# An adaLN transformer block in f32 on one core: the opening of block 0 rearranged (weight sums on GpSimd, modulation ahead of the transposes)

## The chip, the core and the metric

The kernel runs on one core of a Trainium2 chip. A core has a matrix engine (TensorE, PE in the profile, with its weight loads as PEld), VectorE (DVE), ScalarE (ACT), GpSimd (POOL) and SyncE (SP), whose queue here issues nearly all DMAs. The engines run side by side and wait for each other at semaphores; each takes its own instructions strictly in the order in which they were written into its queue. SBUF holds 128 partitions of working memory, PSUM holds the results of TensorE in banks of 128 x 512 f32.

The metric is the device time of one execution in microseconds. A lower time is better.

## The reference

One transformer block over x of 8 x 1024 x 512, with a condition vector for each of the 8 sequences. Everything is f32.

```
mod = silu(condition) @ Wada + bada
sh_a, sc_a, gt_a, sh_m, sc_m, gt_m = split(mod, 6)
xn = layernorm(x) * g1 + be1
xm = xn * (1 + sc_a) + sh_a
q, k, v = split(xm @ Wqkv)                      # 16 heads of 32
attn = softmax(where(causal, q @ k.T * 32 ** -0.5, -inf))
x = x + gt_a * ((attn @ v) @ Wproj + bproj)
xn = layernorm(x) * g2 + be2
xm = xn * (1 + sc_m) + sh_m
x = x + gt_m * (gelu(xm @ W1 + b1) @ W2 + b2)
```

## The kernel before

The 8 x 1024 tokens are worked off as 16 blocks of 512 tokens (two to a sequence). For each block there is a row normalization, a transposition with the modulation (`xm`, four chunks of 128 features by 512 tokens), the three projections k, q and v, the attention in four groups of four heads, the output projection, and the MLP. The order of the instructions is written out by a small planner in Python: every instruction that it emits is noted with an estimated duration, and it picks among several threads of work (the linear work of `plan`, side threads such as the modulation of the next block, the attention) the one that could go on first. Nothing of the order is decided on the chip: each engine executes its own list.

The large linear steps use a Strassen-like scheme (`strassen`, L710): with the weight cut into quarters A11, A12, A21, A22 and the activations into B11, B21, B22 and four derived tiles, a projection takes seven products of 64 matmuls each instead of eight, in the order A11 B11, S2 T2, A12 B21, S1 T1, S3 T3, S4 B22, A22 T4. S1 to S4 are sums of weight quarters, T1 to T4 are differences of activation tiles. T1, T2 and T3 are made on VectorE, T4 on GpSimd (both through `modulated`, L568, with `either` at L148 choosing the engine for T3 and T4). A product's results go from a PSUM bank through `copy_out` (L179) or `combine_out` (L190).

The weight sums are made once. For k, q and v of block 0 (`raw_step`, L282) the four raw quarters are loaded, `weight_sums` (L661) makes S1 to S4, and `keep` (L656) writes each of them to DRAM; for all later blocks the sums are loaded from there. W1 and W2 get theirs from `preparation` (L676), which runs beside block 0.

The weight tiles come in through a ring of nine buffers (`fetch`, L318): a load is issued when the piece nine places earlier has been used for the last time. All loads and all keeps stand in SP's one queue, in the order in which the planner met them.

PSUM is divided into three banks for the linear work (`banks`, L163), a group of four banks `st` for scores and exponentials, and one bank for the attention's output.

What the opening does, in the order of `plan[-1]` (L229): four x tiles of block 0, the eight quarters of two modulation parts (each 256 KB) and then the quarters of k are loaded. The rows of block 0 are normalized (`normalize`, L528: statistics on VectorE, a square root on ScalarE in `root`, L546, and the application of scale and offset to four tiles on ScalarE in `apply`, L553). The step `("at", 0)` transposes them; for block 0 alone the sixteen transposes go into the four banks of `st` (the tile `early`, L610), so that they need no linear bank, and the modulation of their results waits until `norm_columns_a` (L434) has made the gain and shift columns. The step `("mod", 1)` is told to wait for those transposes (`"early"`, L411). Then come k, q, the transposes of block 1 and v.

Of the kernel before, what the change touches and what calls it, by code (L numbers as in the profile page):

```python
# [9 lines left out]
F32 = mybir.dt.float32  # L10
BF16 = mybir.dt.bfloat16
AF = mybir.ActivationFunctionType
# [10 lines left out]
def kernel(  # L23
# [33 lines left out]
    nc = tc.nc  # L57
# [167 lines left out]
    def mlp_steps(n):  # L225
        return [("u", n, i) for i in range(NQ)] + [("d", n, part) for part in range(4)]

    plan = {
        -1: [("at", 0), ("mod", 0), ("mod", 1), ("norm_columns_a",), ("load_xa", 1)]  # L229
        + [("k", 0), ("norm_a", 1), ("q", 0), ("at", 1), ("v", 0)],  # L230
        0: [("load_xa", 2), ("preps",), ("k", 1), ("norm_a", 2), ("gates", "a"), ("q", 1)]
        + [("mod", 3), ("at", 2), ("v", 1), ("mod", 4), ("k", 2), ("gates", "m"), ("columns_m",)],
    }
# [51 lines left out]
    def pieces_of(step):  # L285

        kind = step[0]
        if kind == "mod":
            return [(Wada, step[1], kh, fh) for kh, fh in RAW]
        if kind == "gates":  # L290
            return [(Wada, GATES[step[1]][0], kh, fh) for kh, fh in RAW]
        if kind == "proj":
            return [(Wproj, 0, k) for k in range(NC)]
        if kind == "d":
            return [
                (W2, i, *AT[a]) if a in AT else (W2, i, a)
                for a in DOWN_ORDER[step[2]]
                for i in range(NQ)
            ]
        if raw_step(step):  # L300
            return [(*source_of(step), kh, fh) for kh, fh in RAW]
# [92 lines left out]

    cond_act = tmp.tile([P, TB], F32, tag="top", name="cond_act", bufs=1)[:B, :]
    nc.scalar.activation(cond_act, cond_sb, AF.Silu)
    pc = banks[0][:, : NC * B].rearrange("p (c b) -> p c b", b=B)
    for c in range(NC):
        nc.tensor.transpose(pc[:, c, :], cond_act[:, ts(c, P)], ident[:B, :B])
# [8 lines left out]
    def modulation(i):  # L408
        at = take(4)
        part = {kf: halves(j) for kf, j in zip(RAW, at)}  # L410
        yield ["early"] if i == 1 else [], [BANK]  # L411
        bank = lin_bank()
        pm = banks[bank][:, : NC * B].rearrange("p (c b) -> p c b", b=B)
        for c in range(NC):
            for k in range(NC):
                w = part[k // 2, c // 2][:, k % 2, ts(c % 2, P)]
                matmul(pm[:, c, :], w, condT[:, k, :], k == 0, k == NC - 1, bank=bank)
                note("PE", 90)
                yield [], []
# [23 lines left out]
        return gain, shift  # L443

    columns_of = {}
    written["columns"] = written["early"] = NEVER
    gate_rows = {}

    kept_rows = {}
# [78 lines left out]
    def normalize(tiles, key, sources):  # L528

        for t in range(NTT):  # L530
            written["hat", key, t] = NEVER
        mv = small.tile([P, NTT, 2], F32, tag="mv", name=f"mv_{key}")
        rstd = small.tile([P, NTT], F32, tag="rstd", name=f"rstd_{key}")
        offset = small.tile([P, NTT], F32, tag="offset", name=f"offset_{key}")
        got = []

        def statistics(t):
            st = small.tile([P, nc.vector.BN_STATS_DIM], F32, tag="st", name=f"st_{key}_{t}")
            nc.vector.bn_stats(st, tiles[t])
# [12 lines left out]

        def apply():  # L553
            for t, xt in enumerate(tiles):
                xh = xt
                if key[0] == "m":
                    xh = tmp.tile([P, D], F32, tag="hat", name=f"xh_{key}_{t}", bufs=NTT)
                nc.scalar.activation(
                    xh, xt, AF.Identity, bias=offset[:, t : t + 1], scale=rstd[:, t : t + 1]
                )  # L560
                note_act(800, None, [("rstd", key)], [("hat", key, t)])
                got.append(xh)
            hats[key] = got

        for t in range(NTT):
            add_job(lambda t=t: statistics(t), [sources[t]], key[0] == "m")

    def modulated(key, b, guards):  # L568
# [16 lines left out]
        }  # L585
        xm_of[key] = part
        at = {t: (key, t) for t in part}

        def modulate(c, place, source):
            gain, shift = columns_of[key[0]]  # L590
            writes = [at["B11"], at["T1"]] if c < 2 else [at["B21"], at["B22"]]
            if sooner([source], writes, 770, 780) == "DVE":
                nc.vector.tensor_scalar(
                    xm[:, c, :], place, gain[:, c, b : b + 1], shift[:, c, b : b + 1],
                    ALU.mult, ALU.add,
                )
                note("DVE", 770, [source], writes)
            else:
                nc.scalar.activation(  # L599
                    xm[:, c, :], place, AF.Identity,  # L600
                    bias=shift[:, c, b : b + 1], scale=gain[:, c, b : b + 1],
                )
                note_act(780, None, [source], writes)
# [7 lines left out]
        for c in range(NC):  # L611
            if key != "a0":
                if c:
                    yield [("hat", key, 0)], [BANK]
                bank = lin_bank()
                place, source = banks[bank], ("l", bank)
            else:
                place, source = early[:, c, :], "st"
            for t in range(NTT):
                if t or c:  # L620
                    yield [("hat", key, t)], []
                nc.tensor.transpose(place[:, ts(t, P)], got[t][:, ts(c, P)], ident)  # L622
                note_pe(TR, "whole", [("hat", key, t)], [source])
            if key != "a0":
                modulate(c, place, source)
                live[bank] = False
        if key == "a0":
            written["early"] = 0.0
            yield ["columns"], []
            for c in range(NC):  # L630
                modulate(c, early[:, c, :], "st")
        nc.vector.tensor_tensor(part["T2"], part["B22"], part["T1"], ALU.subtract)  # L632
        note("DVE", 700, [at["B22"], at["T1"]], [at["T2"]], port=True)
        for out, a, b in (("T3", "T2", "B11"), ("T4", "B21", "T2")):
# [26 lines left out]
    def weight_sums(step, part):  # L661
# [3 lines left out]
        got = {"A11": part[0, 0], "A12": part[1, 0], "A21": part[0, 1], "A22": part[1, 1]}  # L665
        for j, (out, a, b, op) in enumerate(SUMS):
            got[out] = stage[:, j, :].rearrange("p (k n) -> p k n", n=HB)
            nc.vector.tensor_tensor(got[out], got[a], got[b], op)
# [28 lines left out]
    def run_preparation(everything=False):  # L697
        while prepared[0] is not None:
# [4 lines left out]
            try:  # L703
                prepared[0][1] = next(prepared[0][0])
            except StopIteration:
                prepared[0] = None

    tail_key = [None]

    def strassen(step, x, dest, target, row, done):  # L710
# [300 lines left out]
    def perform(step):  # L1011
# [2 lines left out]
            yield from modulation(step[1])  # L1014
        elif kind == "norm_columns_a":
            columns_of["a"] = norm_columns("a", 0, 1, O_G1, O_BE1)
            written["columns"] = 0.0
        elif kind == "gates":
            yield from gates(step[1])
        elif kind == "columns_m":  # L1020
# [20 lines left out]
        elif kind == "at":  # L1041
            n = step[1]
            guards = [("m used", n - 3)] if n > 2 else [("v done", 0)] if n == 2 else []
            start(modulated(f"a{n}", blocks[n][0], guards))
        elif kind == "mt":
            n = step[1]
            guards = [("v done", n + 1)]
            start(modulated(f"m{n}", blocks[n][0], guards))
# [492 lines left out]
```

## Time and profile before

| what | value |
|---|---|
| median of 3 runs | 3687.08 us (3687.07 to 3687.18) |
| the profiled execution | 3685.5 us |
| its span (first to last instruction) | 3683.6 us |
| mean granted TensorE clock | 0.992 |
| busy, share of the span: PE, DVE, ACT, POOL | 97%, 59%, 36%, 55% |
| DMA, mean over the span | 117 GB/s |

The opening of block 0 in the same execution, from its timeline:

| us from the start | what |
|---|---|
| 4.85 to 8.83 | SP issues the eight loads of the two modulation parts |
| 8.1 to 12.7 | PE: modulation part 0, as its weights land |
| 11.0 to 12.3 | ACT: table load for the square root |
| 13.0 to 16.0 | ACT: scale and offset applied to four row tiles |
| 13.9 to 19.1 | PE: sixteen transposes |
| 19.0 to 20.7 | PE: modulation part 1 |
| 20.8 to 21.7 | DVE: gain and shift columns |
| 21.8 to 24.6 | ACT: four modulated chunks |
| 22.7 | PE: first product of k |
| 28.5 | PE: second product of k |
| 53.8 | PE: end of q's last product |
| 60.6 to 64.2 | DVE: weight sums of v |
| 77.5 | PE: end of v's last product, k of block 1 begins |

How to read it: busy shares are taken over the whole span. PE's 97% says that it is seldom without an instruction, not that every instruction runs at full rate; the granted clock says that. The clock is granted in steps of 3.41 us, and a step is at full or at half rate. The profile prints it for any stretch as a mean.

### The profile page before, as it was taken

To read this page: it belongs to the slowest core of one execution; us is meant where nothing else is said; L and a number is where in the kernel's file an instruction comes from. 1 tells how busy PE (TensorE), PEld (TensorE's weight loads), DVE (VectorE), ACT (ScalarE), POOL (GpSimd) and SP (SyncE) were. 2 spreads that over 40 slices of the span, in tenths; PEclk is the share of its full clock that TensorE was granted. 3 is DMA by queue.
4 is the path that set the end of the run, shared out by engine and by line. 5 is a ranking of instruction groups with operands and counts; after the bars stand their busy time and mean duration, and the time that the engine had idled before them with its cause. 6 is when DMAs were issued, how large, how long until landed. Compare 5 with 4: busy or idle time off the path is not lost.

```text
span 3683.6 us, 121126 instructions
## 1 busy us (share of the span) xinstructions
PE 3578.0 (97%) x54821; PEld 1770.6 (48%) x54821; DVE 2158.7 (59%) x2455; ACT 1330.8 (36%) x1415; POOL 2030.0 (55%) x2052
## 2 busy tenths in 40 slices
PE   7979999999999999999999999999999999998989
PEld 4424445445454455544545454454544445454445
DVE  5756676564755647465564656646666465664542
ACT  2324334252343523335242352424524244341421
POOL 1676745656456563556636665356653556445661
PEclk9989999999999999999999999999999999999999
DMA  5642333434334343433434333343333433334334
GB/s 182 202 135 90 109 106 105 127 102 130 102 114 119 108 123 110 131 95 107 125 107 139 96 96 119 111 133 102 102 119 111 136 105 108 107 106 123 90 110 133
DMA packets 307893, 430.34 MB, mean 117 GB/s; under 512 B 25900, under 2 KB 176236, under 8 KB 307380
## 3 DMA queue, kind: packets, MB, share of 16 engines
q1 hardware_dynamic: 307264, 422.56, 38.2%
q8 instruction: 432, 7.08, 0.8%
q14 instruction: 81, 0.66, 0.1%
q10 hardware_dynamic: 116, 0.03, 0.0%
HBM read 394.12 MB, written 28.38 MB: 115 GB/s over the span
## 4 chain that ended last, share of the span: by engine, by line
PE 86%; DVE 7%; ACT 2%; POOL 2%; issue 2%; DMA 0%; SPq 0%; ACTq 0%; POOLq 0%; DVEq 0%
PE bank L199 58%; PE st L1292 8%; PE sc L1206 8%; PE po L1343 7%; DVE mx L1226 2%; PE st L1303 2%; PE bank L1361 2%; POOL pT L1427 1%; PE bank L622 1%; ACT pT L1315 1%; DVE hT L928 1%; DVE sc L1218 1%; DVE xr L156 1%; DVE t_m L156 1%; PE bank L1266 0%
## 5 line engine op out<-in xcount | busy, mean ns | idle before, releaser
L1427 POOL TENSOR_TENSOR pT<-pT,pT 128x512 f32<-128x512 f32 (+3 forms) x1280 | 1209.0, 979 | 550.1 <-ACT pT L1315 383.8
L1315 ACT ACTIVATE pT<-st 128x2048 f32<-128x2048 f32 (+1 forms) x320 | 546.6, 1708 | 1019.4 <-PE st L1303 956.9
L199 PE MATMUL bank<-w,hT 128*32 128x256 f32 x14336 | 808.7, 380 | 5.0 <-DVE hT L928 2.2
L1226 DVE TENSOR_REDUCE mx<-sc 128x4 f32<-128x2048 f32 (+3 forms) x384 | 669.0, 1756 | 208.2 <-PE sc L1206 201.6
L199 PEld LDWEIGHTS bank<-w,hT 128*32 128x32 f32 x14336 | 453.2, 110 | 357.9 <-issue 61.3
L199 PE MATMUL bank<-xm_m,w 128*32 128x256 f32 x8192 | 506.4, 380 | 0.8 <-DVE u_u L191 0.8
L1320 POOL TENSOR_SCALAR_AFFINE_SELECT pT<-pT 128x512 f32<-128x512 f32 x256 | 178.1, 708 | 575.2 <-ACT pT L1315 574.9
L199 PE MATMUL bank<-t_m,w 128*32 128x256 f32 x6144 | 383.1, 380 | 2.4 <-DVE t_m L632 1.0
L1292 PE MATMUL st<-qT,kT 32*128 32x512 f32 (+3 forms) x3072 | 342.9, 530 | 35.9 <-DVE mx L1226 34.7
L199 PEld LDWEIGHTS bank<-xm_m,w 128*32 128x32 f32 x8192 | 254.3, 110 | 249.3 <-issue 95.8
L1206 PE MATMUL sc<-kT,qT 32*128 32x512 f32 (+3 forms) x3072 | 340.2, 527 | 12.6 <-DVE mx L1226 6.5
L1343 PE MATMUL po<-pT,v 128*32 128x512 f32 (+3 forms) x3072 | 315.1, 497 | 6.5 <-POOL pT L1320 6.5
L1218 DVE TENSOR_TENSOR sc<-sc,mask 128x512 f32<-128x512 f32 (+1 forms) x192 | 168.0, 875 | 249.4 <-PE sc L1206 221.6
L199 PEld LDWEIGHTS bank<-t_m,w 128*32 128x32 f32 x6144 | 193.0, 110 | 174.3 <-issue 50.2
L199 PE MATMUL bank<-w,qT 128*32 128x512 f32 x2048 | 241.5, 598 | 6.1 <-POOL qT L1381 3.2
L199 PE MATMUL bank<-xm_a,w 128*32 128x256 f32 x3968 | 244.2, 382 | 2.0 <-ACT xm_a L599 2.0
L1376 DVE RECIPROCAL rec<-rec 128x128 f32<-128x128 f32 x256 | 223.7, 918 | 21.6 <-ACT rec L1367 21.6
L1292 PEld LDWEIGHTS st<-qT,kT 32*128 32x128 f32 x3072 | 129.7, 185 | 201.9 <-issue 60.6
L1206 PEld LDWEIGHTS sc<-kT,qT 32*128 32x128 f32 x3072 | 126.7, 184 | 176.0 <-ACT pT L1315 84.7
L191 DVE TENSOR_TENSOR hT<-bank,u_u 128x512 f32<-128x512 f32 x192 | 130.4, 686 | 120.4 <-PE bank L199 118.4
L199 PE MATMUL bank<-t_a,w 128*32 128x256 f32 x2944 | 186.6, 382 | 0.0
L1315 ACT ACT_TABLE_LOAD x88 | 112.9, 1283 | 183.5 <-PE st L1303 182.8
(184 smaller groups left out, 3546.8 us busy)
## 6 DMA issues: line engine op xcount, KB each, us to landing
w<-in_L_cond_W_dram SPq DMA_DIRECT2D x384, 256.0 KB, 2.9
w<-kept_up_S SPq DMA_DIRECT2D x256, 256.0 KB, 2.6
w<-kept_down_S SPq DMA_DIRECT2D x256, 256.0 KB, 2.7
w<-kept_qkv_S SPq DMA_DIRECT2D x180, 256.0 KB, 2.9
w<-in_L_cond_Wqkv_dram SPq DMA_DIRECT2D x147, 256.0 KB, 3.5
hat<-in_x_dram SPq DMA_DIRECT2D x64, 256.0 KB, 3.4
w<-in_L_cond_Wproj_dram SPq DMA_DIRECT2D x64, 256.0 KB, 3.4
xr<-in_x_dram SPq DMA_DIRECT2D x64, 256.0 KB, 4.4
```

The costliest lines, as they stand in the source:

```text
L156: nc.vector.tensor_tensor(out, a, b, op)
L191: nc.vector.tensor_tensor(out, src, other, op)
L199: nc.tensor.matmul(ps[r, :], lhsT[:, r], rhs, start=start, stop=stop, skip_group_check=True)
L1206: nc.tensor.matmul(sc[:, j, c0 : c0 + w], qTs[n][r, g, ts(qt, P)], keys_of(n, kh)[r, g, :w], start=True, stop=True, skip_group_check=True,)
L1218: nc.vector.tensor_tensor(diagonal, diagonal, mask[:, :span].unsqueeze(1).to_broadcast([P, HPG, span]), ALU.add,)
L1226: nc.vector.tensor_reduce(mx[:, kh, qt, :], sc[:, :, c0 : c0 + w], axis=AX.X, op=ALU.max)
L1292: nc.tensor.matmul(st[:, j, c0 : c0 + w], kT[r, g, ts(k % NTT, P)], qT[r, g, TB - w :], start=(c0 == 0), stop=False, skip_group_check=True,)
L1315: nc.scalar.activation(pT[:, :, :used], st[:, :, :used], AF.Exp, scale=scale)
L1320: nc.gpsimd.affine_select(diagonal, diagonal, pattern=[[0, HPG], [1, P]], compare_op=ALU.is_ge, fill=0.0, base=0, channel_multiplier=-1,)
L1343: nc.tensor.matmul(po[r, TB - w :], v[:, k % NTT, g * P + j * hd : g * P + (j + 1) * hd], pT[:, j, c0 : c0 + w], start=(k == 0), stop=last ...
L1376: nc.vector.reciprocal(some, some)
L1427: nc.gpsimd.tensor_tensor(into, into, pT[:, j, c0 : c0 + w], ALU.add)
```

## The change

The diff touches only the opening and the code that it shares with later blocks, whose own steps keep their order. It does this:

- `plan[-1]` is put in another order: both modulation parts first, then a new step `("sums", "k", 0)`, the columns, the transposes of block 0, the loads of block 1's rows, the sums of q, the projection k, and so on; the sums of v stand between q and the transposes of block 1.
- A weight's sums become a step of their own (`sum_weights`), which takes the ring's pieces, and `strassen` picks them up. They are made on GpSimd instead of VectorE. Their keeps move in SP's queue with them.
- An activation with the square root on one column (`warm`) is put behind the silu, so that the table is loaded there.
- Of block 0's four row tiles, two are scaled on VectorE.
- The transposes of block 0 go through the three linear banks like those of the later blocks, and the four-bank tile and its conditions (`early`, `columns`) go.

```diff
     plan = {
-        -1: [("at", 0), ("mod", 0), ("mod", 1), ("norm_columns_a",), ("load_xa", 1)]
-        + [("k", 0), ("norm_a", 1), ("q", 0), ("at", 1), ("v", 0)],
+        -1: [("mod", 0), ("mod", 1), ("sums", "k", 0), ("norm_columns_a",), ("at", 0)]
+        + [("load_xa", 1), ("sums", "q", 0), ("k", 0), ("norm_a", 1), ("q", 0)]
+        + [("sums", "v", 0), ("at", 1), ("v", 0)],
...
     nc.scalar.activation(cond_act, cond_sb, AF.Silu)
+    warm = const.tile([P, 1], F32, tag="warm", name="warm")
+    nc.scalar.activation(warm, eps, AF.Sqrt)
+    table[0] = "sqrt"
...
-        yield ["early"] if i == 1 else [], [BANK]
+        yield [], [BANK]
...
-                nc.scalar.activation(
-                    xh, xt, AF.Identity, bias=offset[:, t : t + 1], scale=rstd[:, t : t + 1]
-                )
-                note_act(800, None, [("rstd", key)], [("hat", key, t)])
+                if key == "a0" and t % 2:
+                    nc.vector.tensor_scalar(
+                        xh, xt, rstd[:, t : t + 1], offset[:, t : t + 1], ALU.mult, ALU.add
+                    )
+                    note("DVE", 700, [("rstd", key)], [("hat", key, t)])
+                else:
+                    nc.scalar.activation(
+                        xh, xt, AF.Identity, bias=offset[:, t : t + 1], scale=rstd[:, t : t + 1]
+                    )
+                    note_act(800, None, [("rstd", key)], [("hat", key, t)])
...
+        for c in range(NC):
+            if c:
+                yield [("hat", key, 0)], [BANK]
+            bank = lin_bank()
+            for t in range(NTT):
+                if t:
+                    yield [("hat", key, t)], []
+                nc.tensor.transpose(banks[bank][:, ts(t, P)], got[t][:, ts(c, P)], ident)
+                note_pe(TR, "whole", [("hat", key, t)], [("l", bank)])
...
-        if key == "a0":
-
-            early = ps_st.tile([P, NC, TB], F32, tag="st", name="early")
...
-            nc.vector.tensor_tensor(got[out], got[a], got[b], op)
-            note("DVE", 700, [], [("sums", *step, out)], port=True)
+            nc.gpsimd.tensor_tensor(got[out], got[a], got[b], op)
+            keys = [("sums", *step, x) for x in (a, b)]
+            note("POOL", 1290, keys, [("sums", *step, out)])
             keep(w, i, out, stage[:, j, :])
...
+    def sum_weights(step):
+        at = take(4)
+        part = {kf: halves(j) for kf, j in zip(RAW, at)}
+        w = weight_sums(step, part)
+        w.update({a: part[kf] for a, kf in AT.items()})
+        summed[step] = at, w
...
         if raw:
-            at = take(4)
-            part = {kf: halves(j) for kf, j in zip(RAW, at)}
-            w = weight_sums(step, part)
+            at, w = summed.pop(step)
```

More of the change, by code (lines that the diff above doesn't have):

```diff
@@ L299, in pieces_of @@
             ]
+        if kind == "sums":
+            return [(*source_of(step[1:]), kh, fh) for kh, fh in RAW]
         if raw_step(step):
-            return [(*source_of(step), kh, fh) for kh, fh in RAW]
+            return []
         if kind in ("k", "q", "v", "u"):
@@ L445 @@
     columns_of = {}
-    written["columns"] = written["early"] = NEVER
     gate_rows = {}
@@ L566, in normalize, with modulated @@
             add_job(lambda t=t: statistics(t), [sources[t]], key[0] == "m")
-    def modulated(key, b, guards):
+    def modulated(key, gain, shift, b, guards):
         for t in ("B11", "B21", "B22", "T1", "T2", "T3", "T4"):
@@ L587, in modulated @@
         at = {t: (key, t) for t in part}
-        def modulate(c, place, source):
-            gain, shift = columns_of[key[0]]
+        for c in range(NC):
[7 more added lines that the diff above has]
+                note_pe(TR, "whole", [("hat", key, t)], [("l", bank)])
             writes = [at["B11"], at["T1"]] if c < 2 else [at["B21"], at["B22"]]
-            if sooner([source], writes, 770, 780) == "DVE":
+            if sooner([("l", bank)], writes, 770, 780) == "DVE":
                 nc.vector.tensor_scalar(
-                    xm[:, c, :], place, gain[:, c, b : b + 1], shift[:, c, b : b + 1],
+                    xm[:, c, :], banks[bank], gain[:, c, b : b + 1], shift[:, c, b : b + 1],
                     ALU.mult, ALU.add,
                 )
-                note("DVE", 770, [source], writes)
+                note("DVE", 770, [("l", bank)], writes)
             else:
                 nc.scalar.activation(
-                    xm[:, c, :], place, AF.Identity,
+                    xm[:, c, :], banks[bank], AF.Identity,
                     bias=shift[:, c, b : b + 1], scale=gain[:, c, b : b + 1],
                 )
-                note_act(780, None, [source], writes)
+                note_act(780, None, [("l", bank)], writes)
+            live[bank] = False
             if c == 1:
@@ L606, in modulate @@
                 note("DVE", 700, [at["B11"], at["T1"]], [at["T1"]], port=True)
-        if key == "a0":
-            early = ps_st.tile([P, NC, TB], F32, tag="st", name="early")
[L611 to L631, printed above, removed]
         nc.vector.tensor_tensor(part["T2"], part["B22"], part["T1"], ALU.subtract)
@@ L706, in run_preparation @@
                 prepared[0] = None
+    summed = {}
+    def sum_weights(step):
[4 more added lines that the diff above has]
+        summed[step] = at, w
     tail_key = [None]
@@ L1016, in perform @@
             columns_of["a"] = norm_columns("a", 0, 1, O_G1, O_BE1)
-            written["columns"] = 0.0
         elif kind == "gates":
@@ L1043, in perform @@
             guards = [("m used", n - 3)] if n > 2 else [("v done", 0)] if n == 2 else []
-            start(modulated(f"a{n}", blocks[n][0], guards))
+            start(modulated(f"a{n}", *columns_of["a"], blocks[n][0], guards))
+        elif kind == "sums":
+            sum_weights(step[1:])
         elif kind == "mt":
@@ L1047, in perform @@
             guards = [("v done", n + 1)]
-            start(modulated(f"m{n}", blocks[n][0], guards))
+            start(modulated(f"m{n}", *columns_of["m"], blocks[n][0], guards))
         elif kind == "k":
```

## The prediction

> **What bounds the kernel now.** I read the page's rows by slice and its chain first, then the chain of waits of the first 100 us, then the stage itself in stretches.
>
> ```profile
> PE   7979999999999999999999999999999999998989
> PE 86%; DVE 7%; ACT 2%; POOL 2%; issue 2%; DMA 0%; SPq 0%; ACTq 0%; POOLq 0%; DVEq 0%
> ```
>
> TensorE is the bound nearly everywhere: 86% of the chain that ended last. Slice 1 (92 us) is only 7 tenths busy, and the change is inside it: the orders of instructions on all five engines are the same in both kernels from about the scores of the second head group on. So the question is how much earlier TensorE gets through the opening.
>
> The chain of waits, start, length, what:
>
> ```profile
> 16.02 3.04 PE early L622 x13
> 19.06 1.69 PE bank L199 x125
> ...
> 25.98 1.76 DVE sums_k L668
> 27.77 0.70 DVE sums_k L668
> 28.52 25.25 PE bank L199 x416
> ...
> 60.62 1.76 DVE sums_v L668
> 62.40 0.70 DVE sums_v L668
> 63.24 7.07 PE bank L199 x96
> ```
>
> Twice TensorE waits for weight sums that VectorE makes late. The first sum takes 1.76 us where the others take 0.7, because GpSimd is in T4 at that moment (same two SBUF operands on each side). From the timeline, the two GpSimd rows that the sum needs, T4 and four weight sums of the later preparation:
>
> ```profile
> 25.43 1.76 POOL L159 TENSOR_TENSOR t_a<-t_a,xm_a 128x512 f32<-128x512 f32 x1 [22.23 <-DVE t_a L632]
> 84.00 5.36 POOL L159 TENSOR_TENSOR prep_up<-prep_up 128x512 f32<-128x512 f32 x4
> ```
>
> The waits cost more than their length. Stretches that I laid on the steps of the granted clock (busy us of PE, PEld, DVE, ACT, POOL, then PEclk, DMA, GB/s):
>
> ```profile
> 20.19:23.60 3.41, 1.40 (x69) 0.74 (x67) 1.15 (x6) 1.77 (x3) 0.00 (x0) 1.00 0.62 175
> 23.60:27.01 3.41, 2.32 (x24) 0.81 (x16) 2.73 (x4) 1.60 (x3) 1.58 (x1) 0.50 0.94 299
> 27.01:30.43 3.42, 1.91 (x20) 0.99 (x24) 2.62 (x4) 0.00 (x0) 0.18 (x1) 0.50 0.90 343
> 30.43:33.84 3.41, 3.41 (x40) 1.58 (x32) 0.69 (x1) 0.00 (x0) 0.00 (x0) 0.50 0.32 115
> 57.73:61.15 3.42, 2.17 (x36) 1.17 (x28) 3.38 (x4) 0.79 (x2) 1.10 (x1) 1.00 0.00 0
> 61.15:64.56 3.41, 1.32 (x25) 0.99 (x29) 3.38 (x5) 0.00 (x0) 0.67 (x1) 1.00 0.38 144
> 64.56:67.97 3.41, 3.41 (x37) 2.13 (x33) 3.38 (x4) 0.00 (x0) 0.00 (x0) 0.50 0.90 296
> ```
>
> A stretch that is 1.40 or 1.32 us busy is followed by one at half clock, one with 2.17 busy is not; and half clock ends only after a stretch that is busy throughout. Before 20 us the rows print 1.00, but the transposes say otherwise: 421 ns each there, 272 ns later. TensorE starts at half rate and gets to full at 20.19.
>
> ```profile
> L622 PE MATMUL early<-ident,hat x16: 421/421/476, 13.9 to 18.6; 128*128 128x128 f32 x16
> L622 PE MATMUL bank<-ident,hat x16: 272/272/331, 53.7 to 56.6; 128*128 128x128 f32 x16
> ```
>
> **The change, part by part.** I rebuild TensorE's schedule to the end of the v projection.
>
> *Order of the plan (mod 1 ahead of the transposes).* The modulation weights' DMAs stand where they stood; the last is issued at 8.35 and its neighbours land 6.2 after issue: 14.6. Half of mod 1 hangs on it: 48 matmuls in 0.83 us (mod 0's row at 11.85), so mod 1 ends at 15.6 instead of 20.7. Gain and shift columns took 1.1 us from there (20.7 to 21.83): ready at 16.7. The 16 transposes follow at 0.234 each (3.04/13, half rate): 15.6 + 3.8 = 19.4.
>
> *Table early, rows on two engines.* Statistics end at 10.92. Without the 1.28 table load and with two rows per engine the rows are done at 11.7 + 2 x 0.73 = 13.2. VectorE's form from SBUF is not in the trace: between 0.18 (128x32) and 0.81 (the same from PSUM); I take 0.7. All of it counts as **nothing**, since TensorE waits for modulation weights until 15.6; the cover is 2.4 us. The new load on ACT (6.5 to 7.8) lies in ACT's 4.55 us of waiting.
>
> *Transposes in the three linear banks.* The fourth needs the first bank back; ACT has it free at 16.9 + 0.78 = 17.7, one 0.94 us step before its turn at 18.5. Nothing. The first product needs two modulated chunks (18.6) and TensorE (19.4): it starts at **19.4, before 22.66**, and ends near 21.5, its first 0.8 us at half rate.
>
> *Sums on GpSimd, a step ahead.* Twelve VectorE instructions go (8.3 us at 0.69), twelve come on GpSimd at 5.36/4 = 1.34. k's last piece needed is issued at 12.5 and lands 4.0 to 6.2 later: 17.6. S1 is done at 19, S2 by 21. T2 then ends the wait: last chunk modulated at 19.4 + 0.1 + 0.78 = 20.3, T2 0.69, and as a two-operand VectorE instruction it now meets a GpSimd sum: 0 to 1.3 us, I take 0.55 (over the whole run the lock costs the instructions of T1's line L605 1.08 in the median and 2.2 at most). Second product: **21.6, before 28.52**. 21.5 to 21.6 is no gap that drops the clock.
>
> At full rate a product is 1.73 us (36.33 to 38.05). Five from 21.6 end at 30.25. The seventh needs T4, which is now queued on GpSimd behind q's four sums: 17.6 + 8 x 1.34 + three locks by T1, T2, T3 of 0.69 + 1.28 = 31.7. A **new wait of 1.4 us** (0 to 2.9 with the landing), too short to drop the clock by the rows above. The rest: 31.7 + 8 x 1.73 = 45.5 against 53.77: **8.3 us**.
>
> *SP's queue.* k's four keeps now stand ahead of block 1's four loads and wait for GpSimd's S4 (25): those loads go at 25 to 27 instead of 23 to 25, land by 31, are wanted by TensorE at 45.5. v's pieces go behind q's keeps (30.2 instead of 42.5), v's sums run 35 to 41. Its four keeps precede k's next pieces (41, wanted at 63). All covered by more than 4 us.
>
> *The v stage*, from q's end E. As before, transposes, first scores and the first product take until E+4.8. Before, v's second product waited for the sums until 63.24 and then ran into half clock; A22 ended at 77.5 = E+23.75. Now: 12 strips, second scores at E+6.1, rest of the product to E+7.6, then 1.73 each, third scores at E+12.4, and 0.8 us of waiting where VectorE's 2.35 us maxima make it late for the last product's bank and the maxima columns: A22 ends at E+19.3. **4.4 us.**
>
> Sum: 8.3 + 4.4 = **12.7 us**. The profiled execution is 3685.5 (span 3683.6 and 1.9 around it); the median is 1.6 above it, so both carry the same opening and I take it off the median: 3687.1 - 12.7 = **3674.4**.
>
> [...] The row first: a gap of 1.95 us (20.7 to 22.66) was followed by half clock. [...] I go by the row, and 1.4 is on the safe side of it.
> [...]
>
> **Rivals.**
> *GpSimd becomes the bound.* For it: T4 took 1.76 under a lock, so sums could. Then T4 ends at 17.6 + 8 x 1.76 + 2.1 + 1.76 = 35.5, a wait of 5.3, with half clock after it: 12.7 - 3.9 - 1.7 = 7.1 us of gain, **3680**. Against: VectorE has only three two-operand instructions in this stretch.
> *The gain is lost later*, **3687**. TensorE idles at 180 to 290 us. Against: the chain there goes scores, maxima, exponential, nothing that keeps an absolute time.
> *Slower, by the clock.* Only the clock's steps stand still while work moves by 12.7 us. The trace has ten half-clock steps of 3.41 us at 184 to 208, 214 to 218 and 273 to 280. Each more costs at most 1.7; it decides from 8 more, and 9 would give **3690**. Against: 12.7 is 3.7 steps, so the work lies nearly as before.
> *The clock helps*: three of the ten go, **3669**.
>
> **How the numbers follow.** Forecast 0.66 (its own range 3671 to 3678), GpSimd 0.12, lost later 0.05, slower 0.05, clock helps 0.12. 0.2% is 7.4 us, the least that a measurement tells here. Faster beyond it (under 3679.7): 0.66 + 0.12 + half of GpSimd's = 0.84; same 0.12; slower 0.04. The range takes in the clock's help and GpSimd's case with the bound of the T4 wait: 3667.5 to 3681.
>
> **What would show it.** First product at 19.4; second at 21.6 without half clock after 23.6; q's end at 45.5; T4 at 31.7 as what the seventh product waits for; no wait for v's sums; k of block 1 beginning 12.7 earlier (64.8 for 77.5), and the same difference at the end. Wrong, if the second product starts after 23.5, if sums take over 1.6 each, or if the difference at 90 us and that at the end are apart by more than 3.

## The result, and the profile after

The change takes 8.1 us off: a median of 3678.70 us in 14 runs (3674.36 to 3683.71) against 3686.82 of the kernel before in 14 runs beside them (3682.46 to 3691.72), a ratio of 0.9978 with an interval of 0.9971 to 0.9985, which is 5.5 to 10.7 us. Forecast were 12.7 us and 3674.4: the size of the likeliest case lies outside the interval. The profiled execution of after took 3678.31 us, its span 3676.6. In both sets runs lie up to 5 us from their median; the three of before that the prediction had seen lay closer together.

The page's rows by slice and its chain by engine, for the kernel after:

```profile
PE   8889999999999999999999999999999999998989
...
PE 86%; DVE 7%; ACT 2%; POOL 2%; issue 2%; DMA 0%; SPq 0%; ACTq 0%; POOLq 0%; DVEq 0%
```

Slice 1 went from 7 to 8 tenths (slices 2 and 3 from 9 and 7 to 8 and 8); the chain has its old shares by engine. The chain of waits of after's first 100 us says why it is not more (start, length, what):

```profile
8.25 5.85 DMA w<-in_L_cond_Wada_dram
14.14 0.30 PE bank L199 x8
14.44 3.06 issue
17.50 0.77 PE bank L199 x40
18.51 1.26 DVE onepa L445
19.99 1.19 DVE shifta L447
21.20 1.19 DVE shifta L448
22.48 0.79 ACT xm_a L616
23.31 1.11 PE bank L606 x4
24.42 25.51 PE bank L199 x448
...
53.05 3.16 PE bank L199 x56
56.22 1.08 PE sc L1208 x16
57.29 5.32 PE bank L199 x96
```

The two waits for weight sums that stood in the chain before are gone, for k as for v. Two things that the prediction does not have stand in front. TensorE stops for 3.06 us inside modulation part 1 with all eight pieces landed and nothing to wait for ("issue"). Then the chain goes through the gain and shift columns on VectorE, three of which take 1.2 us each. In the timeline (start, length, engine, line, operation, what ended the engine's idle time):

```profile
17.50 0.72 PE L199 MATMUL bank<-condT,w 128*32 128x8 f32 x40 [3.06 <-issue]
...
18.46 1.26 POOL L661 TENSOR_TENSOR sums_k<-w,w 128x512 f32<-128x512 f32 x1 [15.28 <-DMA w<-in_L_cond_Wqkv_dram]
18.51 1.25 DVE L445 TENSOR_SCALAR onepa<-modT 128x32 f32<-128x32 f32 x1
19.80 0.19 DVE L446 TENSOR_TENSOR gaina<-onepa,cols 128x32 f32<-128x32 f32 x1
...
19.91 1.26 DVE L447 TENSOR_TENSOR shifta<-onepa,cols 128x32 f32<-128x32 f32 x1
...
21.20 1.18 DVE L448 TENSOR_TENSOR shifta<-shifta,modT 128x32 f32<-128x32 f32 x1
...
25.27 0.69 DVE L625 TENSOR_TENSOR t_a<-xm_a 128x512 f32<-128x512 f32 x1 [1.16 <-ACT xm_a L616]
...
26.00 1.64 DVE L156 TENSOR_TENSOR t_a<-xm_a,t_a 128x512 f32<-128x512 f32 x1
...
29.98 1.29 POOL L159 TENSOR_TENSOR t_a<-t_a,xm_a 128x512 f32<-128x512 f32 x1
```

Each late column ends when a GpSimd sum ends (18.51 + 1.25 = 19.76 beside 18.46 + 1.26 = 19.72; 21.17 beside 21.11, and 22.38 beside 22.34, by the next two sums at 19.80 and 21.08). This is what is called the lock here: a VectorE instruction beside a GpSimd one that ends only with it; no view shows what holds it. Before, the same four took 0.18 to 0.19 each, and modulation 1 ran in one piece:

```profile
18.99 1.69 PE L199 MATMUL bank<-condT,w 128*32 128x8 f32 x128
...
21.00 0.18 DVE L439 TENSOR_SCALAR onepa<-modT 128x32 f32<-128x32 f32 x1
...
21.32 0.18 DVE L441 TENSOR_TENSOR shifta<-onepa,cols 128x32 f32<-128x32 f32 x1
```

The last row of the fence of after shows a mistake of the prediction, and of the section on the kernel before: an instruction that reads `t_a`, then `xm_a`, is T3 = T2 - B11. T4 = B21 - T2 reads them in the other order and is the VectorE row at 26.00. So it is **T3** that stands on GpSimd behind q's four sums, and the fifth product of k needs it, not the seventh. The same holds before the change: the GpSimd row at 25.43, which the prediction calls T4, reads `t_a`, then `xm_a`, and is T3.

### The profile page after: what moved, and what is told of

Read it like the earlier page. It is cut to its first block, busy times and chain, and to the rows that moved or that the text cites. A ratio compares the mean times of both kernels' runs of the same rounds, so it can differ in the third digit from the quotient of the medians.

```text
span 3676.6 us, 121132 instructions
## 1 busy us (share of the span) xinstructions
PE 3575.4 (97%) x54821; PEld 1767.9 (48%) x54821; DVE 2158.9 (59%) x2447; ACT 1327.8 (36%) x1412; POOL 2044.1 (56%) x2064
## 4 chain that ended last, share of the span: by engine, by line
PE 86%; DVE 7%; ACT 2%; POOL 2%; issue 2%; DMA 0%; SPq 0%; ACTq 0%; POOLq 0%; DVEq 0%
PE bank L199 58%; PE st L1294 8%; PE sc L1208 8%; PE po L1345 7%; DVE mx L1228 2%; PE st L1305 2%; PE bank L1363 2%; POOL pT L1429 1%; PE bank L606 1%; ACT pT L1317 1%; DVE hT L929 1%; DVE sc L1220 1%; DVE xr L156 1%; DVE t_m L156 1%; PE bank L1268 0%
```

## The experiments

Times of single kernels can be told apart to some 3 us. The marks of a profile can be told apart to about 1 us (the two profiles of after: 69.36 and 70.17 for the start of block 1's k), so the reading goes by marks. Block 1's k is the last product of the opening's chain; what a kernel gains there agrees with what its median gains to within 2.9 us in all eleven timed experiments, on both signs. The marks are from the timelines of TensorE, in us. The medians of before in the same batches were 3687.34 (rows, columns, whole, columns and whole), 3686.15 (sums on VectorE, before with whole matmuls, v's sums), 3686.02 (all sums, filler, columns with T3) and 3686.34 (the last):

| kernel | stop in modulation | 2nd product of k | 5th product (its wait) | block 1's k | median (runs) | ratio to before, 95% |
|---|---|---|---|---|---|---|
| before | none | 28.52 | 36.33 | 77.52 | | |
| after | 3.06 | 27.32 | 32.50 | 69.36 | 3678.70 (14) | 0.9978 (0.9971 to 0.9985) |
| after, again | 3.38 | 27.33 | 33.30 | 70.17 | 3680.34 (1) | |
| rows and table undone | 3.36 | 27.37 | 32.55 | 69.41 | 3679.25 (10) | 0.9975 (0.9966 to 0.9984) |
| sums on VectorE | 3.22 | 27.12 | 32.30 | 69.89 | 3679.08 (11) | 0.9981 (0.9972 to 0.9990) |
| columns on GpSimd | 3.36 | 25.83 | 33.60 (2.38) | 72.19 | 3680.57 (10) | 0.9978 (0.9968 to 0.9987) |
| whole matmuls | none | 28.44 | 33.62 | 70.51 | 3680.17 (9) | 0.9978 (0.9968 to 0.9988) |
| columns and whole | none | 28.84 | 36.61 (2.38) | 73.51 | 3685.21 (11) | 0.9986 (0.9977 to 0.9995) |
| before, whole matmuls | none | 33.60 | 40.49 | 81.70 | 3690.81 (11) | 1.0010 (1.0001 to 1.0019) |
| before, v's sums ahead | none | 28.09 | 34.98 | 71.85 | 3683.37 (11) | 0.9992 (0.9983 to 1.0001) |
| before, all sums ahead | none | 27.99 | 34.24 (0.78) | 71.13 | 3681.08 (11) | 0.9990 (0.9981 to 0.9999) |
| filler | 2.91 | 24.72 | 31.16 (1.05) | 68.05 | 3677.82 (11) | 0.9978 (0.9970 to 0.9987) |
| columns, T3 | 3.10 | 25.82 | 31.00 | 67.90 | 3677.11 (11) | 0.9975 (0.9966 to 0.9984) |
| columns, T3, filler | 2.59 | 24.47 | 29.64 | 66.54 | 3674.92 (8) | 0.9973 (0.9963 to 0.9984) |

**After, again.** The same kernel in another batch, for a second profile.

> The changed kernel once more: how far its marks in the opening repeat from run to run. Theory: the 3 us gap in modulation part 1 and the lock on the columns come again at the same instructions, block 1's k at 69.4 within 1 us; the whole time may differ by up to 4 us, as the 14 runs did, by the clock's steps further on.

The stop came at the same instruction (216 records of strips before it, 40 behind) and the columns were as late (three of 0.96 to 1.26 us). Neither is an accident of one execution.

**Which parts of the change earn nothing.** First the table and the rows:

```diff
-    warm = const.tile([P, 1], F32, tag="warm", name="warm")
-    nc.scalar.activation(warm, eps, AF.Sqrt)
-    table[0] = "sqrt"
...
-                if key == "a0" and t % 2:
+                if False:
```

> The changed kernel without the early table load and with all four row tiles scaled on ScalarE again. Theory 'both edits are hidden behind the modulation weights': rows done at 16 instead of 13.5, part 1 still ends at 18.2, transposes still start there, all later marks the same, 3678.7. Rival 'the rows set the start of the transposes': everything from there 2.5 us later, 3681.

The four rows are finished at 15.96 instead of 13.46, and the three marks behind the stop move by 0.05 us: what the rows lose is covered by the wait for the modulation. Then the engine of the sums, all twelve still a step ahead:

```diff
-            nc.gpsimd.tensor_tensor(got[out], got[a], got[b], op)
+            nc.vector.tensor_tensor(got[out], got[a], got[b], op)
...
-            note("POOL", 1290, keys, [("sums", *step, out)])
+            note("DVE", 700, keys, [("sums", *step, out)], port=True)
```

> The changed kernel with all twelve sums on VectorE, still as steps of their own ahead of their products. Theory 'the order, a step ahead, earns the gain, and the engine little': no lock on the columns, but k's sums stand ahead of them in VectorE's queue and wait for the last weight until 18.4, then take 4 x 0.69, so columns at 22.3 as with GpSimd; second product 26.5 to 28, block 1's k within 1.5 us of 69.4; 3677 to 3681. Rival 'it is GpSimd that earns it': v waits for its sums again, block 1's k at 72 or later, 3682 or more.

VectorE's timeline of this kernel:

```profile
20.94 0.69 DVE L661 TENSOR_TENSOR sums_k<-w,sums_k 128x512 f32<-128x512 f32 x1
21.54 0.17 DVE L445 TENSOR_SCALAR onepa<-modT 128x32 f32<-128x32 f32 x1
21.75 0.19 DVE L446 TENSOR_TENSOR gaina<-onepa,cols 128x32 f32<-128x32 f32 x1
21.86 0.18 DVE L447 TENSOR_TENSOR shifta<-onepa,cols 128x32 f32<-128x32 f32 x1
```

Each column takes 0.18 again, yet the four are done at 22.2, as in after: they now stand behind k's four sums. That the sums are early is worth something (next test); on which engine they run makes no difference that the marks can tell.

**What the early sums earn without the new order.** To the kernel before, v's sums alone were given as a step ahead on GpSimd, and in a second kernel those of k, q and v:

```diff
-        + [("k", 0), ("norm_a", 1), ("q", 0), ("at", 1), ("v", 0)],
+        + [("k", 0), ("norm_a", 1), ("q", 0), ("sums", "v", 0), ("at", 1), ("v", 0)],
...
```

> The kernel before with one part of the change alone: v's weight sums on GpSimd as a step of their own between q and the transposes of block 1; k's and q's sums stay on VectorE where they were, the opening is untouched. Theory 'the v stage is worth 4.4 us by itself': q's end at 53.8 as before, no wait for v's sums and no half clock after it, block 1's k at 73 instead of 77.5; about 3682.4. Rival 'the gain in v depends on the shorter opening, or is lost to the lock': block 1's k at 76 or later, 3686.

From the end of q's last product (52.43) to block 1's k it takes 19.42 us; before it took 23.75. That is 4.3 us, the predicted 4.4 of the v stage. The median fell by 2.8 us only, with an interval that reaches no change at all, so this rests on the marks.

```diff
-        -1: [("at", 0), ("mod", 0), ("mod", 1), ("norm_columns_a",), ("load_xa", 1)]
-        + [("k", 0), ("norm_a", 1), ("q", 0), ("at", 1), ("v", 0)],
+        -1: [("at", 0), ("mod", 0), ("mod", 1), ("sums", "k", 0), ("norm_columns_a",), ("load_xa", 1)]
+        + [("sums", "q", 0), ("k", 0), ("norm_a", 1), ("q", 0), ("sums", "v", 0), ("at", 1)]
+        + [("v", 0)],
...
```

> The kernel before with all twelve sums on GpSimd a step ahead: the plan's order, the four-bank tile, the table and the rows are as before (four modulated chunks on ScalarE). This undoes the other parts of the change. My theory (the early sums earn nearly all, the order little, since in after its 5 us were given back to the stop of TensorE and to the columns behind the shared port): no stop of TensorE, since its program comes while it transposes; modulation part 1 ends at 20.7; the columns 3 us late behind k's sums, at 24; second product at 28 to 29 (after: 27.3, before: 28.5); fifth at 33 to 35 (T3 at 32); q's end at 51 to 52; block 1's k at 71 to 72 (before 77.5, after 69.4 and 70.2): the time 5 to 6.5 us under before, 1.5 to 2.5 over after. Rival (the order earns what was predicted, some 5 us, and the sums the rest): block 1's k at 74 to 75, the time 3 us under before and 5 over after.

TensorE's timeline of the second kernel:

```profile
18.86 1.90 PE L199 MATMUL bank<-condT,w 128*32 128x8 f32 x128
24.58 3.64 PE L199 MATMUL bank<-xm_a,w 128*32 128x256 f32 x32 [3.83 <-ACT xm_a L604]
...
34.24 1.93 PE L199 MATMUL bank<-t_a,sums_k 128*32 128x256 f32 x32 [0.78 <-POOL t_a L159]
```

No stop (128 records of modulation 1 in one piece), but two columns locked (1.05 and 1.20) and the fifth product waiting for T3. (No view shows the expectation's shared port; the name is that of the kernel's planner, `port=True` in `note`.) Block 1's k starts at 71.13: 6.4 of after's 8.2 us come from the early sums alone. The new order, with table and rows, adds 1.0 to 1.8, where 5.1 earlier microseconds of modulation 1 had been counted. By the medians, which are coarser, the sums alone gain 4.9 of 8.1 us, so that the order would add 3. Either way the rival by which the order earns 5 and block 1's k starts at 74 to 75 falls.

**The stop.** First the modulation's first two parts as 32 matmuls with whole 128-column weights (64 records) in place of 128 strips (256 records), which makes TensorE's program shorter:

```diff
-                matmul(pm[:, c, :], w, condT[:, k, :], k == 0, k == NC - 1, bank=bank)
+                if i < 2:
+                    nc.tensor.matmul(
+                        pm[:, c, :], w, condT[:, k, :],
+                        start=k == 0, stop=k == NC - 1, skip_group_check=True,
+                    )
...
+                else:
+                    matmul(pm[:, c, :], w, condT[:, k, :], k == 0, k == NC - 1, bank=bank)
```

> The changed kernel, but the two modulation parts of the opening use one 128-column matmul where they used four 32-column strips: 32 PE matmul records instead of 128 in each part, same weights, same DMAs, same order on every other engine. Theory 'TensorE had no instructions' (the 3.06 us before the last 40 matmuls of modulation part 1 is the wait for a block of TensorE's program): part 1 ends at 14.5 to 15.2 instead of 18.2, the columns are made before k's sums start on GpSimd (18.4) and so without the lock, 16.1 instead of 22.4; second product of k at 21 to 22 instead of 27.3, q's end at 45 to 46 instead of 49.9, block 1's k at 64.5 to 65.5 instead of 69.4; 4 to 5 us faster than the changed kernel, about 3674. Rival 'a modulation weight landed late and the trace does not show it': part 1 ends at 18 as before, nothing else moves, 3678.7.

```profile
9.89 12.97 PE L424 MATMUL bank<-condT,w 128*128 128x8 f32 x60 [1.06 <-DMA w<-in_L_cond_Wada_dram]
```

The stop is gone, and the run is a miss all the same: a record took 0.22 us in this row (12.97/60) where the four records of strips in its place take 0.07 (4 x 0.72/40 in after), and modulation 1 ended at 22.7. The same edit on the kernel before, to have its price alone:

> Control: the kernel before with the 128-column matmuls in the two modulation parts. Theory 'TensorE lacked instructions only where modulation part 1 follows part 0 at once': here the transposes lie between, the block of its program comes in behind them, and only the shorter part 1 counts: columns 0.5 to 1.3 us earlier, block 1's k 0 to 1.5 us earlier, 3685.5 to 3686.8. Rival 'these strips cost as much in any order': 3 us or more faster.

Against the expectation it made that kernel 4.2 us slower at block 1's k and 4.7 in the median. The edit costs more than the stop, so it cannot price it. The cleaner test leaves the strips alone and puts 24 small matmuls (48 records) ahead of everything on TensorE, with a result that nothing reads:

```diff
+    for _ in range(24):
+        nc.tensor.matmul(
+            banks[2][:32, :8], ident[:, :32], ident[:, :8], start=True, stop=True,
+            skip_group_check=True,
+        )
     pc = banks[0][:, : NC * B].rearrange("p (c b) -> p c b", b=B)
```

> The kernel after with 24 extra small matmuls (identity by eight columns of identity, 48 records, result not read) on TensorE ahead of everything else. My theory: the 3.06 to 3.38 us in which TensorE had landed weights and no waiting instruction, always after 216 of the 256 strip records of the modulation, are a missing block of TensorE's own program, which is fetched by a 16-KB packet on the queue of kind instruction that lies behind the weight loads. Then the stop comes 48 records sooner, after 168 strip records, some 2 to 4 us long, 88 records follow it, and modulation part 1 ends at 17 to 18.5. Rival (the stop belongs to the place: the piece w, its semaphore, the bank or modulation 1): it stays after 216 records with 40 behind it. By either the second product stays within 1.2 us of after's 27.3 and the time within 1.5 us of after.

TensorE's timeline of the kernel with the filler:

```profile
1.42 2.73 PE L404 MATMUL bank<-ident 128*32 128x8 f32 x48 [1.42 <-POOL ident masks.py:199]
...
13.18 0.51 PE L199 MATMUL bank<-condT,w 128*32 128x8 f32 x24 [0.23 <-DMA w<-in_L_cond_Wada_dram]
16.59 1.36 PE L199 MATMUL bank<-condT,w 128*32 128x8 f32 x88 [2.91 <-issue]
...
24.72 1.93 PE L199 MATMUL bank<-t_a,sums_k 128*32 128x256 f32 x32
...
31.16 1.93 PE L199 MATMUL bank<-t_a,sums_k 128*32 128x256 f32 x32 [1.05 <-POOL t_a L159]
```

88 records behind the stop instead of 40: it moved by exactly the 48 that were put in front. So it belongs to a count of TensorE's instructions, not to a piece of weight or a bank. (The filler does not price the stop either: it is still there, and modulation 1 ended only 0.3 us earlier.) What comes at that count is in the DMA view of after from 15 to 16 us (queue and kind: packets, MB, share of the engines' time):

```profile
q1 hardware_dynamic: 346, 0.33, 102.3%
q8 instruction: 1, 0.02, 7.2%
```

One 16-KB packet of kind instruction, among weight loads that keep all DMA engines full (102.3%); the stretch from 14 to 15 has none. It starts at 15.05, 0.6 us after TensorE has stopped, and is in at 16.2, 1.3 us before TensorE goes on. In six of the seven other profiles with a stop the DMA view has one such packet at the stop too; for columns, T3 and filler there is no such view. With whole matmuls, a shorter program, none came between 8 and 26, and there was no stop. In the eight profiles whose modulation runs as strips ahead of the transposes, the stop took 2.59 to 3.38. In the kernel before a packet came at 15.33, while TensorE was in the transposes that the change moved away, and took 1.12. There the same count (128 strips, 16 transposes, 72 strips) is reached at 19.9 (an estimate from the row of modulation 1), 3.5 us after the packet was in, and TensorE did not stop. So by these profiles it takes the count and a packet that is not yet in; that the packet is what TensorE waited for is the reading that fits all of this, and no view shows the wait itself. The second product came 2.6 us earlier with the filler, more than the 1.2 expected: two of the four columns got through before k's first sum began at 18.47, so that all were done at 21.16 instead of 22.38 and the first product began 1.7 us earlier, and it took 1.93 us where in after it took 3.14.

**The columns and T3.** The columns on GpSimd, ahead of k's sums:

```diff
-        -1: [("mod", 0), ("mod", 1), ("sums", "k", 0), ("norm_columns_a",), ("at", 0)]
+        -1: [("mod", 0), ("mod", 1), ("norm_columns_a",), ("sums", "k", 0), ("at", 0)]
...
+        engine = nc.gpsimd if name == "a" else nc.vector
+        engine.tensor_scalar(one_plus, modT[:, ts(gain_at, NC), :], 1.0, None, ALU.add)
...
```

> The changed kernel with the four small column instructions on GpSimd, ahead of k's sums in its queue. Theory 'the lock between VectorE and GpSimd delays the columns': part 1 still ends at 18.2, columns at 19.5 instead of 22.4, the fourth chunk's transposes no longer wait, second product of k at 24.5 to 25.2 instead of 27.3, q's end at 47 to 48, block 1's k at 66.5 to 67.5; 2 to 3 us faster than the changed kernel, about 3676. Rival 'the columns are late only because part 1 is': columns at 22, no difference.

The four take 0.24 to 0.29 each and are done at 20.9; the second product comes 1.5 us earlier, but block 1's k, against the expectation, 2 to 2.8 us later. The timeline, and below it two stretches between steps of the granted clock (busy us of PE, PEld, DVE, ACT, POOL; PEclk, DMA, GB/s):

```profile
32.29 1.26 POOL L159 TENSOR_TENSOR t_a<-t_a,xm_a 128x512 f32<-128x512 f32 x1
...
33.60 3.42 PE L199 MATMUL bank<-t_a,sums_k 128*32 128x256 f32 x32 [2.38 <-POOL t_a L159]
```

```profile
30.47:33.88 3.41, 1.03 (x24) 0.40 (x20) 0.69 (x1) 0.00 (x0) 3.08 (x3) 1.00 1.00 331
33.88:37.29 3.41, 3.41 (x40) 1.69 (x36) 0.22 (x1) 0.00 (x0) 0.00 (x0) 0.50 0.99 350
```

T3 is late by 2.38 us, and the stretch behind it runs at half clock. Columns and whole matmuls together:

> Both together: 128-column modulation matmuls and the columns on GpSimd ahead of k's sums. Theory 'instructions first, lock second': as with the 128-column matmuls alone, within 0.7 us at every mark (second product 21 to 22, block 1's k at 64.5 to 65.5, 3674), since the columns then come before the sums anyway. Rival 'two separate costs that add up': block 1's k 2 us or more earlier than with the matmuls alone.

Neither of the two expectations came true: block 1's k starts 3.0 us later than with whole matmuls alone. It has the same wait of 2.38 us as the columns alone, but here the wait falls across a step of the clock:

```profile
32.39:35.80 3.41, 1.84 (x36) 1.01 (x28) 0.69 (x1) 0.58 (x1) 3.41 (x4) 1.00 1.03 344
35.80:39.21 3.41, 2.60 (x48) 1.59 (x52) 0.59 (x1) 0.00 (x0) 0.76 (x1) 1.00 0.97 330
```

No half clock follows. So here the price of a wait went with where it lay in the 3.41 us stretches: from full clock, 1.03 busy (and 1.40 and 1.32 in the kernel before) was followed by half, 1.84 and more by full. The length alone does not tell: the prediction's gap of 1.95 was followed by half clock, and one of 2.38 once by half and once by full.

Then T3 and T4 of block 0 change engines, beside the columns:

```diff
+            if key == "a0" and out == "T3":
+                nc.vector.tensor_tensor(part[out], part[a], part[b], ALU.subtract)
...
+            elif key == "a0":
+                nc.gpsimd.tensor_tensor(part[out], part[a], part[b], ALU.subtract)
...
```

> The kernel after with the four column instructions on GpSimd ahead of k's sums, and T3 on VectorE with T4 on GpSimd (swapped). My theory: in the kernel after the tile that stands on GpSimd behind q's four sums is T3 (its row reads t_a, xm_a: T2 - B11), which the fifth product of k needs, not T4, which the seventh needs; with the columns alone moved, T3 came 2.38 late and half clock followed. So: second product at 25.8, fifth at 31.0 with no wait, seventh at 34.5 with T4 made at 33.6, q's end 48.4 (after: 49.9, columns alone: 52.8), block 1's k at 68 (after: 69.4 and 70.2; columns alone: 72.2), and the time 1.5 us under that of after, 3 to 4 under that of the columns alone. Rival (the wait is for GpSimd as such, whatever it makes): the wait of 2 to 3 us stays and only moves to the seventh product, block 1's k at 71 to 72. Second rival (the opening's gain is lost later by steps of the clock): block 1's k at 68, and the time as after.

```profile
25.71 1.65 DVE L630 TENSOR_TENSOR t_a<-t_a,xm_a 128x512 f32<-128x512 f32 x1
...
25.82 1.93 PE L199 MATMUL bank<-t_a,sums_k 128*32 128x256 f32 x32 [0.32 <-DVE t_a L626]
...
31.00 1.94 PE L199 MATMUL bank<-t_a,sums_k 128*32 128x256 f32 x32
...
32.29 1.30 POOL L633 TENSOR_TENSOR t_a<-xm_a,t_a 128x512 f32<-128x512 f32 x1
...
34.45 1.94 PE L199 MATMUL bank<-t_a,w 128*32 128x256 f32 x32
```

GpSimd's instruction stands at the same 32.29 and is now T4, wanted at 34.45. The wait is gone, and block 1's k starts 4.3 us earlier than with the columns alone. The rival by which the wait only moves on falls.

**All three.** Columns, T3 and filler in one kernel:

> Columns on GpSimd ahead of k's sums, T3 on VectorE and T4 on GpSimd, and the 24 extra small matmuls ahead: the three costs found in the opening, each taken off or thinned. My theory (they add up): the stop after 168 strip records, modulation part 1's end at 18 (19.3 without the extra matmuls), columns done at 19.4, first product at 21.6, second at 24.5, no wait at the fifth or the seventh, q's end 47, block 1's k at 66.5 (columns and T3 without the extra matmuls: 67.9; after: 69.4 and 70.2), the time 1.4 under that of columns and T3, some 3 under that of after: 3675.5 against a before of 3686. Rival (the 1.3 us go into a new wait: T4 behind eight sums that now start at 19.5 and end past 31, or S2 itself at 24): the second product at 25 or later, or a wait at the seventh, block 1's k at 67.5 to 68, the time as with columns and T3.

```profile
16.68 1.36 PE L199 MATMUL bank<-condT,w 128*32 128x8 f32 x88 [2.59 <-issue]
...
24.47 1.93 PE L199 MATMUL bank<-t_a,sums_k 128*32 128x256 f32 x32
...
66.54 1.91 PE L199 MATMUL bank<-xm_a,w 128*32 128x256 f32 x32
```

Second product and block 1's k are where they were expected, 11.0 us before the kernel before and 2.8 before after. Its median is 3674.92 us, 11.4 under that of before beside it. Against after it is the better one by the marks; by the medians the two intervals overlap.

## Why the prediction was right, and where it was not

- **The direction and the range held**, and the likeliest case's size did not: 8.1 us against 12.7. 3678.70 lies just above that case's own range of 3671 to 3678. That the whole range took it in is in part luck: its upper end was set for GpSimd as the bound, which is not what happened.
- **Modulation 1's end: 15.6 forecast, 18.2 found.** The strips themselves went as forecast: the eight before the stop ended at 14.44 and the other 40 took 0.72. The term missed is the stop of 3.06; the last piece landed 0.5 earlier than forecast.
- **Columns: 1.1 forecast, 4.1 found** (18.3 to 22.4). The lock of VectorE by a GpSimd sum was priced for T2, which it missed (0.69), and not for the columns, which are small but stood beside k's sums (three took 1.18 to 1.26 in place of 0.18 to 0.19).
- **Transposes: 0.234 each forecast, 0.235 found** (2.82/12). "Nothing" for the linear banks failed in after (the fourth chunk waited 2.34 us for the modulation of an earlier one), as a consequence of the late columns: with the columns on GpSimd all sixteen go in one piece.
- **The second product: 21.6 forecast, 27.32 found.** Modulation 1 came 2.6 us late. The late columns added the 2.34 that the transposes waited (the rest of their 3.0 was covered), and the first product took 2.97 to the start of the second where 2.2 were forecast: 0.8. (Its 32 records took 3.14 where the second's took 1.90; in the kernel before, 3.64 goes with a printed clock of 0.50, though for this stretch of after the profile prints 1.00.) Together that is the difference of 5.7. By the prediction's own mark (later than 23.5) this step is wrong.
- **The step that failed most was the name T4.** GpSimd's last piece was forecast for 31.7 and came at 31.27. That this agrees is in part luck: k's sums began at 18.46 instead of 17.6, and the eight sums took 11.6 us with their locks instead of 12.8. But the piece is T3, needed two products earlier. With the forecast's own numbers the fifth product would have been due at 26.8 and held until 31.7, and q's end would have been 31.7 + 10 x 1.73 = 49.0, not 45.5: 4.8 us where 8.3 was said. So 3.5 of the 4.5 us that are missing were not to be had with T3 there, however early the second product came. The filler kernel shows it: 2.6 us earlier at the second product, 1.05 of waiting at the fifth, 1.3 earlier at block 1's k. By the same sum, stop and lock cost after only what T3 leaves, an estimate of 32.50 - 31.27 = 1.2 us. Had the forecast known T3 there, its own terms would have given 4.8 + 4.4 = 9.2 us of gain, before any half clock behind so long a wait; 8.1 were measured.
- **q's end: 8.3 forecast, 3.83 found** (49.94 against 53.77). **The v stage: 4.4 forecast, 4.33 found** (69.36 - 49.94 = 19.42 against 23.75), with v's sums at 36.1 to 41.2 where 35 to 41 was said.
- **Sums: 1.34 forecast**; 1.26 to 1.31 for k's, and 1.72, 1.77, 1.73 and 1.29 for q's, the first three of which lie beside T1, T2 and T4 on VectorE. By the prediction's mark (over 1.6 each) these three are wrong: each took some 0.45 more than k's.
- **Table and rows at nothing: right**, by the experiment. The rows on two engines were done at 13.46 (13.2 forecast).
- **The rivals.** GpSimd as the bound was given 7.1 us of gain and 0.12, by slower sums. The mechanism is real in four of the kernels here (a wait in the column of the fifth product), but through the tile that it makes last, and not in after itself, where T3 was in 1.2 us before its product. So the measured 8.1, nearer to that rival's 7.1 than to 12.7, does not speak for it. Nothing was lost later: 8.2 us at block 1's k, 8.1 at the end. No slower case showed. The slower rival takes the clock's steps to stand still: those laid at 30.47 in the columns kernel fit the steps of the kernel before (20.19 + 3 x 3.41 = 30.42), those at 32.39 in columns and whole do not. The 1.7 us that is taken for a step at half clock is half of 3.41, an estimate, and no run shows it by itself: columns, with a wait of 2.38 and one step at half clock behind it, began block 1's k 4.3 us later than columns with T3.

What stays open: what the stop alone costs, since no test took it away without another cost; when the instruction packet was asked for, and whether it would come sooner under thinner weight traffic; holding back the weight loads was not tried.

## What to carry to other kernels

Before a wait is priced, read from the operands in their order which tile the row makes, and count from it to its consumer; the same instruction, at the same 32.29, was harmless as T4 and as T3 cost a wait of 2.38 us with a stretch at half clock behind it. Where work is moved to another engine, list what the receiving engine's queue and its locks will hold up, small instructions too (here columns of 0.18 us took up to 1.30). Where a long, dense run of small TensorE instructions is put under the heaviest DMA traffic, look in the trace for stops that nothing shown explains (2.59 to 3.38 us here), and for instruction packets beside them.

## What was not expected of the hardware

- TensorE stopped for 2.59 to 3.38 us with nothing to wait for in any view, always after 216 strip records, or after 168 with 48 other records put ahead; in after a 16-KB instruction packet lay in the stop, while the DMA engines moved 351 GB/s.
- A 128x32 instruction on VectorE took up to 1.30 us in place of 0.18 beside a GpSimd sum of 128x512, and ended with the sum (in after within 0.06 us); the one with a single tensor operand (`onepa`, 1.25) as much as those with two.
- A matmul with 128 weight columns and eight moving columns in f32 took 0.22 us a record (12.97/60), three times the four records of 32-column strips in its place (4 x 0.72/40 = 0.07).
- One and the same wait of 2.38 us was followed by half clock in one kernel (0.50 in the stretch from 33.88 to 37.29 of columns) and by full clock in another (1.00 from 35.80 to 39.21 of columns and whole).
